# Graph attention and graph convolution on one core: values by a second level of seven products, and two weights in one tile

## Chip, core and metric

The kernel runs on one core of a Trainium2 chip. The time is device microseconds of one execution; three runs are shown. A profile of one more execution gives the trace.

## What is computed

```python
# x: (32, 512, 512) f32, adj: (512, 512) of 0 and 1, weights (512, 512), 8 heads of 64
def attention(x):
    q, k, v = x @ Wq + bq, x @ Wk + bk, x @ Wv + bv      # split into 8 heads
    scores = q @ k.T / sqrt(64) + where(adj == 0, -1e9, 0)
    return softmax(scores) @ v
def convolve(x):
    d = where(deg > 0, rsqrt(deg), 0)                     # deg: row sums of adj
    return (adj * d[:, None] * d[None, :]) @ (x @ weight) + bias
x = layernorm(x + attention(x))
x = layernorm(x + convolve(x))
```

Everything is float32. One of the 32 elements of the first axis is called a batch below.

## The kernel before

Every projection of a batch is a product of two 512 x 512 matrices, and each is made by seven products of their halves in place of eight (Strassen's scheme in Winograd's form). The tile `XT` (seven parts of 128 x 2 x 256, the 2 being two blocks of the contracted axis) holds the transposed x: parts 0 to 3 are its quadrants, parts 4 to 6 and a rewritten 2 are differences. `wk`, `wq`, `wv`, `w1` hold the weights in the same seven parts. `seven` (line 315) walks a table of steps: a bank of PSUM (region A, B or D), the numbers of the two parts, and the moves afterwards, either "put" (a copy to SBUF by ScalarE) or "add" (VectorE adds the bank to what lies in SBUF). A later step on the same region goes on adding up in the bank, so it must wait until the moves have read it. `values_of` (line 335) has one half product per step, four matmuls of 128 x 128 by 256 columns. `CHAIN` (line 288) is its table: products (0,0), (4,4), (5,5), (1,1), (6,6), (2,3), (3,2).

The order of instructions on each compute engine is written out by hand: `InOrder` (line 34) pins it, and `play(main, beside)` (line 104) runs one entry of `main`, which are matmul steps with their moves, and then the side work listed under its number. The DMAs of SP are issued through the scheduler, in order, and wait for what they need.

The main loop (line 777) handles batch b with its neighbours b+1 (projections), b-1 and b-2 (convolution and the second normalization):

- `stretch(b, one)`, line 452: scores of two head pairs (tile `sc`; VectorE masks into `e`, ScalarE takes the exponential in place), POOL's sums of numerators (`accumulate`, tile `acc`, three adds a head pair), then the product of numerators and values (`av`); VectorE transposes that into the one buffer `yb`, from which four DMAs fill `yT`. Eight tiles `e` rotate.
- keys and queries of b+1, two chains of seven steps taken in turn (`kq`), with beside them on POOL and ScalarE the second normalization's factors and output (`rstd`, `add`, then `y`, stored by SP) of b-2, and the first normalization of b-1.
- `stretch(b, two)` for the other two head pairs.
- `conv["first"]` of b-1 (adjacency by `hi` and `lo`), `values_of(b + 1)`, and `conv["second"]` of b-1, again seven half products. Beside them: `turn` (line 126) transposes x of b+2 into `XT` in two halves on VectorE; the first turn frees the x buffer, and `load_x` on SP then fetches the second half. `combine` (line 159) makes the four differences on POOL, and `bias_values` (line 357) adds the bias to the values on POOL. In this version POOL does the bias first and the differences afterwards.

Iterations 0, LAST-1 and LAST have orders of their own. `wv` and `wq` stand in tiles of their own for the whole kernel; late in the kernel free parts of them serve as scratch (lines 419, 485, 681).

Of the kernel before, what the change touches and what calls it, by code (L numbers as in the profile page):

```python
# [1 line left out]

# [15 lines left out]
P = 128  # L18
# [31 lines left out]
def unshifted(  # L50
# [24 lines left out]
    consts = ctx.enter_context(tc.tile_pool(name="consts", bufs=1))  # L75
    acts = ctx.enter_context(tc.tile_pool(name="acts", bufs=2))
    work = ctx.enter_context(tc.tile_pool(name="work", bufs=2))
    small = ctx.enter_context(tc.tile_pool(name="small", bufs=3))
    psum = {}

# [29 lines left out]

    X = {}
    columns = consts.tile([P, 12, 2, DT], F32, name="columns")
    XT = consts.tile([P, 7, 2, HALF], F32, name="xT")

    def load_x(b, j):
        if b == 1 and j == 1:
            X[b, j] = work.tile([P, 8, DT, 32], F32, name="x1", tag="e", bufs=8)
        else:
            X[b, j] = acts.tile([P, 8, DT, 32], F32, name="x", bufs=1)
        for q in range(4):  # L120
            nc.sync.dma_start(
                X[b, j][32 * q : 32 * (q + 1)],
                x[b, ts(j, HALF), ts(q, P)].rearrange("(k s) (t r) -> s k t r", s=32, r=32),
            )
# [34 lines left out]
    def combine(b, at):  # L159
        to, a, c = PARTS[at]  # L160
        engine = gpsimd if b else vector
        engine.tensor_tensor(XT[:, to], XT[:, a], XT[:, c], ALU.subtract)

    R = {}

# [42 lines left out]
    R[0] = acts.tile([P, NT, D], F32, name="xr", tag="zT", bufs=1)  # L208
    R[0] = [R[0][:, i, :] for i in range(NT)]

    wv = consts.tile([P, 7, 2, HALF], F32, name="wv")
    for i in range(2):
        for k, engine in enumerate((nc.sync, nc.scalar)):
            engine.dma_start(R[0][2 * i + k], x[0, ts(2 * i + k, P), :])
# [3 lines left out]
    wk = load_parts(Wk, "wk", nc.sync)  # L218
    bk_c = load_column(bk, 0)
    bq_c = load_column(bq, 1)  # L220
    wq = load_parts(Wq, "wq", nc.sync)
    adj_sb = acts.tile([P, NT, N], F32, name="yT")
    nc.sync.dma_start(adj_sb, adj.rearrange("(t p) o -> p t o", p=P))
    w1 = consts.tile([P, 7, 2, HALF], F32, name="w1")
    for i in range(2):
# [2 lines left out]
            W1[:, ts(i, HALF)].rearrange("(t p) o -> p t o", p=P),  # L228
        )
    b1_r = load_row(b1, "b1_r", nc.sync)  # L230
    load_x(1, 0)
    load_x(1, 1)

# [78 lines left out]
        ("A", (6, 6), (("add", (1, 1)), ("put", (1, 0)))),  # L312
        ("E", (3, 2), (("add", (1, 0)),)),
    )
    def seven(table, multiply, put, add):
        regions = {}

        def step(region, ij, moves):
            fresh = region not in regions
            if fresh:  # L320
                regions[region] = bank([P, 2, HALF])
            p = regions[region]
            multiply(p, *ij, fresh)
            for kind, q in moves:
                (put if kind == "put" else add)(q, p)

        return each(step, *table)
# [5 lines left out]
        vector.tensor_scalar(bias[:, 1], bq_c, SCALE, None, op0=ALU.mult)  # L333

    def values_of(b):
        def multiply(p, i, j, fresh):
            for r in range(2):
                for u in range(2):
                    tensor.matmul(
                        p[:, r, :], XT[:, j, u, ts(r, P)], wv[:, i, u, :],  # L340
                        start=fresh and r == 0 and u == 0, stop=u == 1, skip_group_check=True,
                    )

        def out(i, j):
            if b not in V:
                V[b] = acts.tile([P, NT, D], F32, name="v", bufs=1)
            return V[b][:, 2 * j : 2 * j + 2, ts(i, HALF)]

        def put(q, p):
            scalar.copy(out(*q), p)  # L350

        def add(q, p):
            vector.tensor_add(out(*q), out(*q), p)

        return seven(CHAIN if b else PLAIN_FIRST, multiply, put, add)

    def bias_values(b):
        for n in range(NT):
# [1 line left out]

    def keys_and_queries(b, r):
        def multiply(p, i, j, fresh):
            for c, w in enumerate((wk, wq)):
                for u in range(2):
                    tensor.matmul(
                        p[:, c, :], w[:, i, u, ts(r, P)], XT[:, j, u, :],
                        start=fresh and c == 0 and u == 0, stop=u == 1, skip_group_check=True,
                    )

        def out(i, j):  # L370
            if (b, ORDER[0]) not in KQ:
                for g in ORDER:
                    KQ[b, g] = acts.tile([P, 2, N], F32, name="kq", bufs=6)
            return KQ[b, r + 2 * i][:, :, ts(j, HALF)]

        def put(q, p):
            g = r + 2 * q[0]
            for c in range(2):
                scalar.activation(out(*q)[:, c], p[:, c], AF.Identity, bias=bias[:, c, g : g + 1], scale=1.0)

        def add(q, p):
            vector.tensor_add(out(*q), out(*q), p)

        return seven(CHAIN if b else PLAIN_FIRST, multiply, put, add)
# [5 lines left out]
    def scores(b, g):  # L390
        E[b, g] = []
        for j in range(NT):
            e = work.tile([P, 2, N], F32, name="e", bufs=8)
            E[b, g].append(e)
            p = pair("sc")
            for k in range(2):
                r = slice(k * HD, (k + 1) * HD)
                tensor.matmul(p[:, k, :], KQ[b, g][r, 0, ts(j, P)], KQ[b, g][r, 1, :], start=True, stop=True)
            vector.scalar_tensor_tensor(
                e, p, CUT, maskT[:, j, None, :].to_broadcast([P, 2, N]), op0=ALU.min, op1=ALU.subtract  # L400
            )
            scalar.activation(e, e, AF.Exp)

    def accumulate(b, g):
# [9 lines left out]
        for l in range(2):  # L414
            n = 2 * ORDER.index(g) + l
            if n < 2:
                a = work.tile([P, 2, N], F32, name="acc", bufs=2)
            else:
                t, at = ((XT, 0), (XT, 2), (XT, 4), (wv, 0), (wv, 2), (wv, 4))[n - 2]
                a = t[:, at : at + 2].rearrange("p k u o -> p k (u o)")  # L420
            gpsimd.tensor_add(a, e[2 * l], e[2 * l + 1])
            ACC[b, g].append(a)
# [53 lines left out]
    def sums(b, c, p):  # L476
# [5 lines left out]
                    start=k == 0, stop=k == len(parts) - 1,  # L482
                )
        if c == 0:
            SM[b] = wq[:, 6].rearrange("p u n -> p (u n)")
            vector.tensor_scalar(SM[b], p, 1e-36, None, op0=ALU.max)
        else:
            vector.scalar_tensor_tensor(SM[b], p, 1e-36, SM[b], op0=ALU.max, op1=ALU.add)
# [137 lines left out]
    def convolve(b):  # L626
# [48 lines left out]
        def multiply(p, i, j, fresh):  # L675
            if "y" not in t:
                if last:
                    t["y"] = [work.tile([P, 2, D], F32, name="y2", tag="e", bufs=8) for _ in range(2)]
                else:
                    if b == LAST - 2:  # L680
                        y = wq[:, :NT].rearrange("p k u o -> p k (u o)")
                    else:
                        y = acts.tile([P, NT, D], F32, name="y", tag="lo", bufs=1)
                    t["y"] = [y[:, 2 * k : 2 * k + 2, :] for k in range(2)]
# [9 lines left out]
        def move(q, p, to):  # L694
            if not aside:
                vector.tensor_add(of(t["y"], *q), to(*q), p)
                return
            side = work.tile([P, 2, HALF], F32, name="side", tag="e", bufs=8)
            scalar.copy(side, p)
            extend.append(lambda: gpsimd.tensor_add(of(t["y"], *q), to(*q), side))  # L700

# [54 lines left out]
    turn_first(1, 0)  # L756
    turn_first(1, 1)
    run(v[1:5])
    scalar.activation(wq[:, :4], wq[:, :4], AF.Copy, scale=SCALE)
    weigh(wk, gpsimd)  # L760
    run(v[5:])
    biases()
    wq_parts = each(lambda k: weigh_part(wq, vector, k), *range(4))
    kq = keys_and_queries(0, 0)
    run(wq_parts[:2] + kq[:1] + wq_parts[2:3] + kq[1:2] + wq_parts[3:] + kq[2:])
    bias_values(0)
    play(keys_and_queries(0, 1), {
        1: [lambda: adjacency(0)], 3: [lambda: turn(1, 0), lambda: adjacency(1)],
# [1 line left out]
    turn(1, 1)  # L770
    for k in range(4):
        combine(1, k)

    f, c = {}, {}
    for b in range(B):
# [13 lines left out]

        def turns(b=b + 2):
            if b >= B:
                return [], []
            return [lambda: turn(b, 0)], [lambda: turn(b, 1)] + [lambda k=k: combine(b, k) for k in range(4)]

        fold0, fold1 = folds(one) if b < LAST else ([], [])
        rest = back["measure"][3:] + back["root"] if back else []
# [21 lines left out]
        else:  # L820
# [5 lines left out]
                3: conv["parts"][1:] + e["inverse0"] + ahead["grow"],  # L826
            })

        stretch(b, two, f[b]["pairs"][0] + f[b]["pairs"][1] if b == LAST else ())

        fold0, fold1 = folds(two) if b < LAST else ([], [])
        turn0, turn1 = turns()
        if b < LAST:
            end = f[b]
            v, bias_v = values_of(b + 1), [lambda b=b + 1: bias_values(b)]
            if b == 0:
                play(v, {
                    1: fold0, 4: turn0 + fold1, 6: bias_v + turn1,
                })
            else:  # L840
                conv = c[b - 1]
                main = conv["first"] + v + conv["second"]
                grow, parts, scale = ahead["grow"], conv["parts"], end["scale"]
                if b < LAST - 1:
                    beside = {
                        1: parts[:1] + fold0, 3: parts[1:], 4: fold1, 5: grow[:1], 6: grow[1:2] + end["inverse"],
                        7: grow[2:3] + scale[:1], 8: grow[3:] + scale[1:2] + turn0, 9: scale[2:3],
                        10: scale[3:] + bias_v, 12: turn1,
                    }
                else:  # L850
                    measure, norm, low = end["measure"], end["norm"], end["low"]
                    beside = {
                        0: [lambda: load_residual(LAST - 1)], 1: parts[:1] + fold0, 3: parts[1:], 4: fold1,
                        5: grow[:1] + end["inverse"], 6: grow[1:2] + scale[:2], 7: grow[2:3] + scale[2:] + end["add"],
                        8: grow[3:], 9: measure[:1], 10: measure[1:2] + bias_v, 11: measure[2:3],
                        12: measure[3:] + end["root"], 13: norm[:1], 14: norm[1:2] + low[:1], 15: norm[2:3] + low[1:2],
                        16: norm[3:] + low[2:3], 17: low[3:] + end["lift"],
                    }
                play(main, beside)

# [311 lines left out]
```

## Time and profile before

| | us |
|---|---|
| median of 3 runs | 2747.85 (2747.67 to 2747.91) |
| profiled execution | 2747.42 |
| its span, first to last instruction | 2745.6 |
| mean granted TensorE clock | 0.998 |
| busy TensorE, VectorE, POOL, ScalarE | 2720.6, 1890.6, 1792.8, 1260.1 |

In the profile PE is TensorE's matmul side and PEld its weight loads; DVE is VectorE, ACT ScalarE, POOL GpSimd, SP the engine that issues DMAs. All instructions that go through the recording helper carry its line, 44, so groups are told apart by their tiles, written out<-in. A float32 matmul appears as two records, a float32r matmul (`hi`, `lo`) as one. In a timeline the columns are start, length, engine, line, operation, tiles, shape and count, and in brackets the idle time before and what ended it. Matmuls overlap, so the pace is the distance between starts, not the length of one. DMA moved 141.04 MB at a mean of 51 GB/s.

### The profile page before, as it was taken

The page shows a single profiled execution, that of the slowest core. Times are in us where ns is not written, and L with a number is a line of the kernel's source. Part 1 is how long each engine was busy: PE and PEld are TensorE (multiplying, and loading weights), DVE is VectorE, ACT ScalarE, POOL GpSimd, SP SyncE. Part 2 cuts the span into 40 slices and gives each one's busy share as a digit, 9 for nine tenths or more (in the row PEclk, how much of TensorE's full clock was granted, in tenths as well). Part 3 has the DMA queues.
Part 4 walks back from the last instruction along what each step waited for, and adds up shares of the span by engine and source line. Part 5 has one row for each costly group of instructions (what it writes and reads, how often), then busy time and mean ns, then how long its engine had stood idle before and what let it go on. Part 6 is the DMA issues. An engine that isn't in the chain of part 4 may idle for free.

```text
span 2745.6 us, 34622 instructions
## 1 busy us (share of the span) xinstructions
PE 2720.6 (99%) x12540; PEld 1900.4 (69%) x12540; DVE 1890.6 (69%) x2685; ACT 1260.1 (46%) x1807; POOL 1792.8 (65%) x1176
## 2 busy tenths in 40 slices
PE   9999999999999999999999999999999999999997
PEld 6676676776766766767667677676676676766765
DVE  4777766667666667666777666766666766677667
ACT  3335444454444454444544445444445544454444
POOL 4666667567676666666666756667666666667665
PEclk9999999999999999999999999999999999999999
DMA  4111221112121111211122211212111121112211
GB/s 127 31 28 46 58 58 47 54 39 54 54 62 39 45 48 54 62 43 45 45 58 58 50 50 39 54 55 62 39 46 47 54 62 43 48 41 58 64 38 47
DMA packets 379107, 141.04 MB, mean 51 GB/s; under 512 B 277808, under 2 KB 345392, under 8 KB 378928
## 3 DMA queue, kind: packets, MB, share of 16 engines
q1 hardware_dynamic: 377776, 137.17, 19.0%
q8 instruction: 101, 1.65, 0.3%
q10 hardware_dynamic: 1152, 1.57, 0.2%
q14 instruction: 78, 0.64, 0.1%
HBM read 71.83 MB, written 33.55 MB: 38 GB/s over the span
## 4 chain that ended last, share of the span: by engine, by line
PE 97%; DVE 2%; ACT 0%; DMA 0%; issue 0%; POOL 0%; SPq 0%; DVEq 0%; POOLq 0%; ACTq 0%
PE mm L44 64%; PE sc L44 16%; PE av L44 16%; DVE xT L44 0%; DVE st L44 0%; DVE yT L44 0%; DMA xr<-in_x_dram 0%; POOL y L44 0%; ACT yT L44 0%; ACT hi L44 0%; DVE y L44 0%; DMA x<-in_x_dram 0%; DVE mv L44 0%; DVE folded L44 0%; DVE acc L44 0%
## 5 line engine op out<-in xcount | busy, mean ns | idle before, releaser
L44 ACT ACTIVATE e<-e 128x1024 f32<-128x1024 f32 x512 | 541.1, 1057 | 493.2 <-DVE e L44 460.0
L44 DVE SCALAR_TENSOR_TENSOR e<-sc,maskT 128x1024 f32<-128x1024 f32 x512 | 584.8, 1213 | 107.5 <-PE sc L44 107.5
L44 POOL TENSOR_TENSOR acc<-acc,e 128x1024 f32<-128x1024 f32 x248 | 589.3, 2376 | 19.4
L44 PE MATMUL mm<-xT,wk 128*128 128x256 f32 x1792 | 463.2, 381 | 0.3 <-DVE kq L44 0.3
L44 PE MATMUL sc<-kq 64*128 64x512 f32 x2048 | 459.7, 597 | 1.8 <-DVE e L44 1.4
L44 PE MATMUL mm<-xT,wq 128*128 128x256 f32 x1792 | 459.9, 379 | 0.0
L44 PE MATMUL av<-e,v 128*64 128x512 f32 x2048 | 453.6, 595 | 0.3
L44 POOL TENSOR_TENSOR acc<-e 128x1024 f32<-128x1024 f32 x126 | 298.0, 2366 | 233.7 <-ACT e L44 233.7
L44 PE MATMUL mm<-wv,xT 128*128 128x256 f32 x1792 | 398.1, 380 | 0.6 <-DVE xT L44 0.6
L44 PEld LDWEIGHTS mm<-xT,wk 128*128 128x128 f32 x1792 | 337.5, 190 | 70.5 <-DVE mv L44 23.5
L44 PEld LDWEIGHTS mm<-xT,wq 128*128 128x128 f32 x1792 | 340.5, 190 | 46.3
L44 PEld LDWEIGHTS mm<-wv,xT 128*128 128x128 f32 x1792 | 338.0, 190 | 47.9 <-issue 1.4
L44 PEld LDWEIGHTS sc<-kq 64*128 64x128 f32 x2048 | 191.5, 186 | 238.1 <-issue 175.1
L44 PEld LDWEIGHTS av<-e,v 128*64 128x64 f32 x2048 | 145.0, 137 | 301.4 <-issue 264.4
L44 ACT ACTIVATE kq<-mm,bias 128x256 f32<-128x256 f32 x512 | 214.5, 473 | 284.6 <-PE mm L44 284.4
L44 POOL TENSOR_TENSOR v<-v,bv_r 128x512 f32<-128x512 f32 x128 | 161.3, 1288 | 239.2 <-ACT v L44 236.5
L44 POOL TENSOR_TENSOR yT<-yT,b_r 128x512 f32<-128x512 f32 x126 | 156.9, 1278 | 241.1 <-DVE lo L44 241.1
L44 DVE STREAM_TRANSPOSE yb<-av 128x512 f32<-128x512 f32 x127 | 91.1, 717 | 253.9 <-DMA yT<-yb 202.9
L44 PE MATMUL mm<-w,zT 128*128 128x256 f32 x992 | 229.6, 379 | 0.0
L44 PEld LDWEIGHTS mm<-w,zT 128*128 128x128 f32 x992 | 188.3, 190 | 26.6 <-issue 1.1
L44 PE MATMUL mm<-adjT,hi 128*128 128x512 f32 x512 | 201.5, 397 | 0.8 <-ACT side L44 0.8
L44 PE MATMUL mm<-adjT,lo 128*128 128x512 f32 x512 | 197.8, 390 | 0.0
(121 smaller groups left out, 3000.0 us busy)
## 6 DMA issues: line engine op xcount, KB each, us to landing
yT<-yb SPq DMA_DIRECT2D x508, 64.0 KB, 2.3
x<-in_x_dram SPq DMA_DIRECT2D x248, 128.0 KB, 2.5
out_dram<-y SPq DMA_DIRECT2D x123, 256.0 KB, 2.0
xr<-in_x_dram SPq DMA_DIRECT2D x118, 256.0 KB, 3.3
wk<-in_x_dram SPq DMA_DIRECT2D x8, 256.0 KB, 2.8
wk<-in_L_gnn_Wk_dram SPq DMA_DIRECT2D x8, 128.0 KB, 4.5
wq<-in_L_gnn_Wq_dram SPq DMA_DIRECT2D x8, 128.0 KB, 3.1
yT<-in_adj_dram SPq DMA_DIRECT2D x1, 1024.0 KB, 6.9
```

What stands on the lines that cost most here:

```text
L44: return self.tc.keep_in_program_order(op(*args, **kwargs))
```

## The change

In batches 1 to 31 the four half products (1,1), (3,2), (2,3), (4,4) of the values are each made by seven products of quarters. One leaf step does the same quarter product of all four, as four matmuls of 128 x 128 by 128 columns, into one bank. Three half products, (0,0), (5,5), (6,6), follow as before (`OUTER`), now all as adds. The product (4,4) has to reach two quadrants, which one add on POOL does (`spread_last`).

For that, x needs four more parts of quarters (`quarter`, on POOL, four adds a batch, `XT` grows from 7 to 11 parts), and the weights need three (`weigh_quarters`, once, at the start). The seven parts of `wv` and of `wq` are written to DRAM once and share the tile `wqv`: `swap(1)` loads the values' weights after the keys and queries, `swap(0)` brings the queries' back after the values. The eight numerators become one tile `NUM`, taken in the same rotation; its first four slots hold `wv` during the start. Turns, combinations, quarters and bias adds take new places, and `conv["second"]` is interleaved with the last values' steps.

```diff
+    def numerators():
+        return NUM[:, next(taken) % 8]
+    def quarter(at):
+        old, new = XT[:, 1:5].rearrange("p k u (t o) -> p k u t o", t=2), QUARTERS
+        to, a, c = (
+            (1, old[:, :, 0, 1], old[:, :, 0, 0]), (2, old[:, :, 1, 1], new[:, 1]),
+            (3, old[:, :, 1, 1], old[:, :, 0, 1]), (0, old[:, :, 1, 0], new[:, 2]),
+        )[at]
+        gpsimd.tensor_tensor(new[:, to], a, c, ALU.subtract)
...
+    def swap(k):
+        nc.sync.dma_start(wqv, stored[k])
...
+    LEAF = tuple(CHAIN[k] for k in (0, 1, 3, 2, 5, 4, 6))
+    OUTER = (
+        ("A", (0, 0), (("add", (0, 0)),)),
+        ("A", (5, 5), (("add", (0, 1)),)),
+        ("A", (6, 6), (("add", (1, 1)), ("add", (1, 0)))),
+    )
...
+        def multiply_quarters(p, i, j, fresh):
+            for n, (k, l) in enumerate(((1, 1), (3, 2), (2, 3), (4, 4))):
+                right = w[:, k, i % 2, ts(i // 2, P)] if i < 4 else wv_quarters[:, i - 4, k - 1]
+                left = XT[:, l, j % 2, ts(j // 2, P)] if j in (0, 1, 3) else QUARTERS[:, max(j - 3, 0), l - 1]
+                tensor.matmul(p[:, n, :], left, right, start=fresh and n == 0, stop=True, skip_group_check=True)
+        def put_quarters(q, p):
+            out(0, 0)
+            scalar.copy(quarter_of(*q), p.rearrange("p (j i) o -> p j i o", i=2))
+        def add_quarters(q, p):
+            to = quarter_of(*q)
+            vector.tensor_add(to, to, p.rearrange("p (j i) o -> p j i o", i=2))
+        def spread_last():
+            gpsimd.tensor_add(out(0, 1), out(0, 1), out(1, 1))
...
-        return seven(CHAIN if b else PLAIN_FIRST, multiply, put, add)
+        if b == 0:
+            return seven(PLAIN_FIRST, multiply, put, add)
+        leaf = seven(LEAF, multiply_quarters, put_quarters, add_quarters, (4, P))
+        return leaf + [spread_last] + seven(OUTER, multiply, put, add)
...
+    weigh_quarters(gpsimd)
+    nc.sync.dma_start(stored[1], NUM[:, :4].rearrange("p e k (u o) -> p (e k) u o", u=2)[:, :7])
+    nc.sync.dma_start(stored[0], wqv)
     bias_values(0)
...
-            return [lambda: turn(b, 0)], [lambda: turn(b, 1)] + [lambda k=k: combine(b, k) for k in range(4)]
+            return [lambda: turn(b, 0)], [lambda: turn(b, 1)], [lambda k=k: combine(b, k) for k in range(4)] + [quarters]
...
+        if b < LAST:
+            swap(1)
         stretch(b, two, f[b]["pairs"][0] + f[b]["pairs"][1] if b == LAST else ())
...
+            back_to_queries = [lambda: swap(0)] if b < LAST - 1 else []
             if b == 0:
                 play(v, {
-                    1: fold0, 4: turn0 + fold1, 6: bias_v + turn1,
+                    1: fold0, 4: fold1, 8: turn0, 9: turn1, 10: combined + back_to_queries + bias_v,
                 })
...
-                main = conv["first"] + v + conv["second"]
+                second = conv["second"]
+                k = 6 if b < LAST - 1 else 8
+                main = conv["first"] + v[:k] + second[:1] + v[k:9] + second[1:2] + v[9:10] + second[2:3] + v[10:] + second[3:]
...
-                        1: parts[:1] + fold0, 3: parts[1:], 4: fold1, 5: grow[:1], 6: grow[1:2] + end["inverse"],
-                        7: grow[2:3] + scale[:1], 8: grow[3:] + scale[1:2] + turn0, 9: scale[2:3],
-                        10: scale[3:] + bias_v, 12: turn1,
+                        1: parts[:1] + fold0, 3: parts[1:], 5: fold1, 6: grow[:1], 8: grow[1:2], 9: grow[2:3] + end["inverse"],
+                        10: grow[3:] + scale[:1], 11: scale[1:2], 13: turn0 + scale[2:3], 14: scale[3:],
+                        16: turn1, 17: combined[:2], 18: combined[2:] + back_to_queries + bias_v,
```

Iteration LAST-1 gets a new list of side work in the same manner, with `k` 8 in place of 6. The scratch that lay in `wv` and `wq` moves to `wqv` and, for the second convolution of batch LAST-2, to the quarters' parts of `XT`.

## Prediction

> **What bounds the kernel now.** I read the page first, then TensorE's timeline of one batch, then those of the other engines over the same batch.
>
> ```profile
> span 2745.6 us, 34622 instructions
> PE 2720.6 (99%) x12540; PEld 1900.4 (69%) x12540; DVE 1890.6 (69%) x2685; ACT 1260.1 (46%) x1807; POOL 1792.8 (65%) x1176
> PE 97%; DVE 2%; ACT 0%; DMA 0%; issue 0%; POOL 0%; SPq 0%; DVEq 0%; POOLq 0%; ACTq 0%
> L44 PE MATMUL mm<-wv,xT 128*128 128x256 f32 x1792 | 398.1, 380 | 0.6 <-DVE xT L44 0.6
> L44 PEld LDWEIGHTS mm<-wv,xT 128*128 128x128 f32 x1792 | 338.0, 190 | 47.9 <-issue 1.4
> ```
>
> TensorE sets the end (97% of the chain of waits); every other engine has idle time. A float32 product is two records, so 1792 is 32 batches of 7 products of 4 matmuls. A mean of 380 ns is a latency; the pace must come from the spacing in TensorE's timeline:
>
> ```profile
> 39.59 1.04 PE L44 MATMUL mm<-ident,yT 128*128 128x128 f32 x8
> 40.47 1.03 PE L44 MATMUL mm<-xT,wk 128*128 128x256 f32 x4
> ...
> 134.75 0.38 PE L44 MATMUL mm<-folded,spread 128*128 128x128 f32 x2
> 134.97 1.03 PE L44 MATMUL mm<-xT,wk 128*128 128x256 f32 x4
> ...
> 1193.47 5.34 PE L44 MATMUL mm<-wv,xT 128*128 128x256 f32 x24
> 1198.65 0.38 PE L44 MATMUL mm<-folded,spread 128*128 128x128 f32 x2
> ```
>
> From 1193.47 to 1198.65, 24 records of 256 columns: 0.216 us each, a half product of 8 records 1.727. Records of 128 columns: 0.88/8 = 0.110 (transposes), 0.22/2 = 0.110 (folded).
>
> Batches repeat every 84.42 us. I give times of a batch from S, the start of the first stretch's scores (1217.96). Keys and queries start at S+14.08. The change loads POOL, which ScalarE waits for, so these rows (POOL, then ACT) matter most:
>
> ```profile
> 1206.64 4.99 POOL L44 TENSOR_TENSOR v<-v,bv_r 128x512 f32<-128x512 f32 x4 [7.89 <-ACT v L44]
> 1211.58 5.20 POOL L44 TENSOR_TENSOR xT<-xT 128x512 f32<-128x512 f32 x4
> 1222.71 2.37 POOL L44 TENSOR_TENSOR acc<-e 128x1024 f32<-128x1024 f32 x1 [5.94 <-ACT e L44]
> ...
> 1237.26 1.02 POOL L44 TENSOR_TENSOR rstd<-ve,minus_half 128x4 f32<-128x4 f32 x1
> 1238.36 0.20 POOL L44 TENSOR_TENSOR add<-nmu,rstd 128x4 f32<-128x4 f32 x1
> ```
>
> ```profile
> 1238.59 0.81 ACT L44 ACTIVATE y<-y,add,rstd 128x512 f32<-128x512 f32 x1 [1.95 <-POOL add L44]
> 1239.31 0.82 ACT L44 ACTIVATE kq<-mm,bias 128x256 f32<-128x256 f32 x2
> ...
> 1242.15 0.84 ACT L44 ACTIVATE kq<-mm,bias 128x256 f32<-128x256 f32 x2
> ```
>
> POOL is free from 1216.78 (S-1.2) to 1222.71 (S+4.75), then sums numerators without a break, then makes the norm factors. ScalarE stands 1.95 us for them, with the bank copies of keys and queries queued behind. The third copy of the first chain ends at 1242.99 (S+25.03). Its bank is needed again by that chain's fifth product, the ninth step, which TensorE starts at 1245.96 (S+28.0). The slack is 2.95 us.
>
> **The change, part by part.**
>
> *Smaller products.* Out go 4 half products a batch: 32 x 0.216 = 6.91 us. In come 7 x 4 matmuls, 56 records x 0.110 = 6.16. That is -0.75 us in each of batches 1 to 31, -23 us in all. No row has 56 such records in line. From below I take 0.109, from above the mean weight load of 190 ns, as if no load overlapped more than its neighbour; I take 0.110, since the folded pair has real float32 loads of 190 ns and still keeps 0.110. The Trainium skill ("TensorE: Matmul & The Clock Gate", section "Back-to-back issue gap") speaks against this part: it gives a sustained 81 ns for a pair of weight load and matmul at 128 columns, where the stream alone would be about 56. An estimate by that ratio is 0.155 us a record here, 8.7 us a batch, a loss of 1.8; the two rows at 0.110 don't agree with it, but they are short.
>
> *Moves out of PSUM.* The seven small products have 4 copies on ScalarE (0.59) and 3 adds on VectorE (0.69), as CHAIN had; the three outer ones add 4 adds on VectorE, 2.6 us. A small product takes 0.88 us of TensorE, so a bank is wanted back sooner. The closest is the seventh after the sixth on the same bank: the add is done 0.27 + 0.65 us after the sixth, and a `second` product of 1.73 us stands between. Hidden. In batch LAST-1 nothing stands between but the folded pair: about 0.8 us, once.
>
> *Weights in turn.* Two DMAs of 1.8 MB a batch, on SP. The adjacency (1 MB) took 6.9 us beside other loads; by that, 12 us. Values may wait 14.2 + 7.2 us after the last query product, the queries 6.9 + 14.1 after the last value product, iteration 0 has 14.2. Hidden; from above, twice as slow, 3 us late at each swap. Behind the swap on SP stand yT<-yb (issued 11.5 us after a stretch's start) and x loads for the next round; neither is short of time. The numerators keep their ring of eight.
>
> *POOL and the order of turns.* This decides. Before, the bias adds (4) and combinations (4) ran from S-11.3 to S-1.2. Now both x turns come later: turn one after the first outer product, turn two after the third of the `second` products. Behind turn two stand on POOL 4 combinations, 4 quarters and 4 bias adds; the spread add goes into idle time. The turns wait for each other through the load of the second half of x, which SP issues when turn one has freed the buffer. In iteration 0 that load ended the wait:
>
> ```profile
> 113.49 1.24 DVE L44 STREAM_TRANSPOSE xT<-x 128x1024 f32<-128x1024 f32 x1
> ...
> 118.87 1.25 DVE L44 STREAM_TRANSPOSE xT<-x 128x1024 f32<-128x1024 f32 x1 [1.17 <-DMA x<-in_x_dram]
> ```
>
> 4.14 us lie between the end of one and the start of the other. After the first outer product TensorE still has eight products of 1.727 and 0.1 us to S, so it ends at S-13.9. Its add waits 0.27 and takes 0.6; turn one ends 1.24 later, at S-11.8; turn two starts 4.14 later and ends at S-6.4; POOL starts at S-6.3. Behind turn two on VectorE stand the last outer product's adds and the next `second` adds; no bank of theirs is wanted for two products (3.5 us).
>
> A POOL add of 512 elements runs 1.27, one every 1.235, or 1.345 behind its own result (the four xT: 5.20). Twelve, five of them behind a result, take 15.4 us to the start of acc: S+9.1 instead of S+4.75, 4.35 late. For the quarters, four runs of 128, the nearest rows are 1.27 (whole) and 1.42 (y<-y,side, two runs of 256, mean); nothing is below. I take 1.27; 1.42 adds 0.6 us. The bias adds end at S+5.4 to S+9.1, one every 1.24; the attention product starts at S+7.1 and needs the last of them at S+9.7: free by 0.6. But acc, rstd and add are POOL's own line, so ScalarE's store starts 4.35 later, the third copy ends at S+29.4, and TensorE, ready at S+28.0, waits **1.4 us a batch**. After that the chain recovers: the last low part ends at S+39.4, b1's adds at S+44.4, as the second stretch's acc starts (S+44.6).
>
> So a batch changes by -0.75 + 1.43 = +0.68.
>
> *Iteration 0*, with no `second` to stand between: VectorE ends the second yb at 106.5, folds to 109.0, adds twice to 110.1, folds to 112.5, adds to 113.1. The seventh small product starts then instead of at 109.1. Scores start at 119.3 (116.16 before); turn one ends 117.9, turn two 123.3; POOL's twelve run 123.4 to 138.8, so the last values of the first head pair end at 139.7, of the second at 143.3. Keys start there instead of 132.92: +10.4, less 0.75 in the next values: +9.6 once.
>
> *Startup*: the weights' quarters (4 adds, 5 us) lie in POOL's idle 20.3 us before 52.8; quarters of batch 1 delay acc by 5 there, with 13 us idle behind. Nothing.
>
> **Sum.** 9.6 + 28 x 0.68 (iterations 2 to 29) + 1.5 (iteration 30: 0.68 and 0.8) = +30. The span becomes 2775.6, and with the 1.8 us around it (profiled execution 2747.42) 2777.5; the median of the runs is 0.4 above that execution.
>
> **Rivals.**
> - *The gain comes through.* POOL's line reaches ScalarE less than 2.95 us late, for instance if the quarters take 0.9 us or the x load lands sooner. For it: 35% of POOL is idle. Against: the rows above. 9.6 + 0.8 - 29 x 0.75 = -11.4: 2736. The kernel is faster than before from a line 1.05 us shorter on (a wait under 0.39), and all of it is there at 1.4.
> - *The line is longer.* Quarters of 1.43 us (the mean of w<-w, POOL's slowest adds of this size) and an x load 1.2 us later, 1.8 us more a batch: +50, about 2828. For it: a line without slack passes every delay on.
> - *Weight loads bind.* 56 x 0.19 = 10.6, +3.7 a batch in place of -0.75, about 2907. Or the swaps land 3 us late twice a batch, about 2950. Against: 0.110, and 20 us of cover.
> - *The change does less than it says*: a wait of 0.3 to 0.65 instead of 1.43, near 2750, so that gain and waits cancel.
>
> **How the numbers follow.** Forecast 0.58 (2764 to 2800: quarters at 1.42 give +17, and the start of the line, which rests on one load's 4.14 us, may be 0.2 to 0.45 us off, 6 to 13 us in 29 batches); gain comes through 0.20; near 2750 0.07; longer line 0.10; weight loads or swaps 0.05. Less or more than 0.2% (5.5 us) is about what a measurement of this kernel can tell from no change: faster 0.20, same 0.07, slower 0.73. The range 2734 to 2805 leaves out part of the first rival, most of the longer line and the last.
>
> **What would show it.** In TensorE's timeline the small products at 0.88 us each; POOL's acc at S+9; ScalarE's first y near S+25; a gap of about 1.4 us in TensorE before the ninth step of keys and queries, put down to ScalarE's kq; batches 85.1 us apart; iteration 0's values with a wait of 4 us. Wrong if that gap is missing, or if gaps stand before the first value or query product (DMA), or the small products are wider than 0.9 us.

## The result, and the profile after

| | before | after |
|---|---|---|
| median of 4 runs each, us | 2747.88 (2747.67 to 2748.88) | 2786.28 (2785.86 to 2788.38) |
| profiled execution, its span, us | 2747.42, 2745.6 | 2788.38, 2786.6 |
| mean granted TensorE clock | 0.998 | 0.995 |

The ratio is 1.0141 [1.0123, 1.0158]: the kernel became 38 us slower, where 30 were forecast. The profiled execution of after is the longest of its four runs, 2.1 us over their median, so the account below, made against it, explains 41 us. 1.2 of them lie behind TensorE's last product, at the very end of that execution, as is said further down.

The page of after, in the places that answer to those of before: span, busy times, chain by engine, and the groups of the first key products and of the values.

```profile
span 2786.6 us, 36220 instructions
PE 2717.3 (98%) x13284; PEld 1907.6 (68%) x13284; DVE 1972.3 (71%) x2809; ACT 1257.0 (45%) x1807; POOL 1999.4 (72%) x1335
PE 76%; DVE 8%; POOL 5%; ACT 4%; DMA 3%; SPq 2%; issue 1%; ACTq 0%; DVEq 0%; POOLq 0%
L45 PE MATMUL mm<-xT,wk 128*128 128x256 f32 x1792 | 466.5, 383 | 32.5 <-ACT kq L45 32.5
L45 PE MATMUL mm<-wqv,xT 128*128 128x128 f32 x1736 | 304.8, 322 | 5.8 <-DVE v L45 5.8
```

TensorE still sets the end, but its part of the chain fell from 97% to 76%: other engines now end waits that it stands in. One row says which. The products of keys and queries stood 32.5 us for ScalarE's `kq`, and the view of waits counts them:

```profile
PE mm L45 <- ACT kq L45: 32.5, 29, 1.6
```

29 times, once a batch. The next three views, POOL, ScalarE and TensorE, follow one such wait back to its start. They are timelines of the batch whose first scores start at S = 1242.03.

```profile
1235.84 10.38 POOL L45 TENSOR_TENSOR xT<-xT 128x512 f32<-128x512 f32 x8 [7.04 <-DVE xT L45]
1246.17 4.98 POOL L45 TENSOR_TENSOR v<-v,bv_r 128x512 f32<-128x512 f32 x4
1251.11 2.37 POOL L45 TENSOR_TENSOR acc<-e 128x1024 f32<-128x1024 f32 x1
...
1266.59 0.20 POOL L45 TENSOR_TENSOR add<-nmu,rstd 128x4 f32<-128x4 f32 x1
```

```profile
1266.83 0.81 ACT L45 ACTIVATE y<-y,add,rstd 128x512 f32<-128x512 f32 x1 [6.11 <-POOL add L45]
1267.55 0.82 ACT L45 ACTIVATE kq<-mm,bias 128x256 f32<-128x256 f32 x2
...
1270.38 0.84 ACT L45 ACTIVATE kq<-mm,bias 128x256 f32<-128x256 f32 x2
```

```profile
1269.17 1.03 PE L45 MATMUL mm<-xT,wqv 128*128 128x256 f32 x4
1271.28 1.13 PE L45 MATMUL mm<-xT,wk 128*128 128x256 f32 x4 [1.08 <-ACT kq L45]
```

POOL waits 7.04 us for the second x turn, starts its twelve adds at S-6.2 and reaches `acc` at S+9.1 without a pause. `add` comes 4.2 us later than before, ScalarE stands 6.11 us for it (1.95 before) in front of its first `y`, the third copy ends at S+29.2, and TensorE, ready at S+28.0, waits. The step after the wait starts its records a little further apart as well (1.13 in place of 1.03 for the group).

The shift of after against before, by stage, in the two profiled executions:

| | forecast | measured |
|---|---|---|
| to the first scores of iteration 2 | +9.6 | +14.0 |
| 28 batches (iterations 2 to 29) | +19.0 | +23.0 |
| iteration 30 to the end | +1.5 | +3.9 |
| sum | +30 | +41 |

### The profile page after: what moved, and what is told of

The parts are those of the page before. It is cut to its first block, busy times and chain, and to the rows that moved or that the text cites. A ratio compares the mean times of both kernels' runs of the same rounds, so it can differ in the third digit from the quotient of the medians.

```text
span 2786.6 us, 36220 instructions
## 1 busy us (share of the span) xinstructions
PE 2717.3 (98%) x13284; PEld 1907.6 (68%) x13284; DVE 1972.3 (71%) x2809; ACT 1257.0 (45%) x1807; POOL 1999.4 (72%) x1335
## 4 chain that ended last, share of the span: by engine, by line
PE 76%; DVE 8%; POOL 5%; ACT 4%; DMA 3%; SPq 2%; issue 1%; ACTq 0%; DVEq 0%; POOLq 0%
PE mm L45 48%; PE sc L45 15%; PE av L45 13%; POOL acc L45 2%; ACT kq L45 2%; DMA yT<-yb 2%; SPq L512 2%; ACT y L45 1%; DVE yb L45 1%; DVE folded L45 1%; DVE acc L45 1%; DVE ve L45 1%; POOL rstd L45 1%; POOL xT L45 1%; DVE st L45 1%
## 5 line engine op out<-in xcount | busy, mean ns | idle before, releaser
L45 PE MATMUL mm<-xT,wk 128*128 128x256 f32 x1792 | 466.5, 383 | 32.5 <-ACT kq L45 32.5
L45 POOL TENSOR_TENSOR xT<-xT 128x512 f32<-128x512 f32 x250 | 314.2, 1273 | 243.2 <-DVE xT L45 233.4
L45 PE MATMUL mm<-xT,wqv 128*128 128x256 f32 x1792 | 459.9, 379 | 0.0
L45 PEld LDWEIGHTS mm<-xT,wqv 128*128 128x128 f32 x1792 | 340.5, 190 | 46.3
L45 PE MATMUL mm<-wqv,xT 128*128 128x128 f32 x1736 | 304.8, 322 | 5.8 <-DVE v L45 5.8
L45 PEld LDWEIGHTS mm<-wqv,xT 128*128 128x128 f32 x1736 | 263.4, 192 | 30.0 <-issue 4.6
L45 DVE TENSOR_TENSOR v<-v,mm 128x512 f32<-128x512 f32 x221 | 147.5, 679 | 151.0 <-PE mm L45 146.3
L45 DVE STREAM_TRANSPOSE acc<-acc 128x1024 f32<-128x1024 f32 x124 | 152.6, 1231 | 77.1 <-POOL acc L45 76.8
## 6 DMA issues: line engine op xcount, KB each, us to landing
x<-in_x_dram SPq DMA_DIRECT2D x244, 128.0 KB, 3.2
```

The costliest lines, as they stand in the source:

```text
L45: return self.tc.keep_in_program_order(op(*args, **kwargs))
```

## The experiments

Theory: POOL's line between the second x turn and `acc` has become longer than the slack that ScalarE and the banks of keys and queries leave, and what is over goes to TensorE's wait before the ninth step, batch by batch; the first values of iteration 0 add a once-only cost. Rivals: POOL's load as such, the swaps of weights, the pace of the small products. Every ratio is to the kernel before, run on the same chip.

**The quarters made later** (`e1_quarters_late`): the same four adds, after the norm factors instead of ahead of `acc`.

```diff
-            return ..., [lambda k=k: combine(b, k) for k in range(4)] + [quarters]
+            return ..., [lambda k=k: combine(b, k) for k in range(4)]
-                        7: weights[2:3], 8: exact[2:3], 9: weights[3:], 10: exact[3:],
+                        7: weights[2:3], 8: exact[2:3], 9: weights[3:] + [quarters], 10: exact[3:],
-                        4: store[3:] + measure[:2], 5: measure[2:] + ahead["root"], 7: ...
+                        4: store[3:] + measure[:2], 5: measure[2:] + ahead["root"] + [quarters], 7: ...
```

> The four quarters adds of each batch leave POOL's line ahead of acc and run during keys and queries of the same XT, after rstd and add of the first normalization, where POOL stood idle 7.6 us; all work is kept. Theory (POOL's line of twelve makes ScalarE late, and TensorE waits for ScalarE): the line shrinks by 5.1 us, acc starts near S+4.8, the gap before the ninth step of keys and queries is gone, batches 83.85 us apart (84.43 - 0.60), iteration 0 about 5 us shorter; about 2744 us. Rival 1 (the swaps or the small products themselves hold things up): nothing moves but a little of the start, 2775 or more. Rival 2 (POOL's total load counts, not the place): within 10 us of the changed kernel's 2786.

Measured: 2741.95 us, ratio 0.9979 [0.9970, 0.9989]. POOL's timeline in the batch with S = 1219.03:

```profile
1218.01 4.96 POOL L45 TENSOR_TENSOR v<-v,bv_r 128x512 f32<-128x512 f32 x4
1223.73 2.37 POOL L45 TENSOR_TENSOR acc<-e 128x1024 f32<-128x1024 f32 x1 [0.77 <-ACT e L45]
```

The bias adds are done 0.77 us before the exponentials are there, so `acc` starts at S+4.7 (4.8 before the change), and the ninth step starts at S+28.0 with no wait. POOL's busy time rose all the same, from 1999.4 to 2028.8 us. Its load isn't the cause; the place of four adds is.

**Only the fourth quarter made later** (`e2_one_late`).

```diff
-        for at in range(4):
+        for at in range(3):
             quarter(at)
+    def last_quarter():
+        quarter(3)
-                        ..., 5: measure[2:] + ahead["root"], 7: ...
+                        ..., 5: measure[2:] + ahead["root"] + [last_quarter], 7: ...
```

> One of the four quarter adds (the fourth) is made while keys and queries run, after acc and the norm factors; the other three stay ahead of acc. Theory (a threshold: the wait before the ninth step is what POOL's line is longer than the slack): the line is one add shorter, 1.24 to 1.35 us, so acc starts near S+7.7, the third copy of the first chain ends near S+27.8, and the wait of 1.15 us is gone in ordinary batches; 0.1 to 0.7 us of it is left in the about five batches whose x load lands late. The gain of 0.60 a batch then comes through in iterations 2 to 29: 15 to 17 us of loss less 23 to 25 in after, about 2750 to 2755 us (the start and the tail still cost 14 and 4). Rival (POOL's load as such slows the kernel, in proportion): a quarter of what moving all four gave, 44.3/4 = 11 us, about 2775.

Measured: 2750.15 us, ratio 1.0006 [0.9997, 1.0016]. `acc` starts at S+7.8, the third copy ends at S+28.0, and the whole row of 32.5 us has shrunk, in the waits of this kernel, to

```profile
PE mm L45 <- ACT kq L45: 2.2, 5, 0.6
```

One add of 1.27 us a batch is worth 36 us here: a threshold, not a load.

**Two quarters made twice** (`e6_two_more`): the second and third are computed again, with the same values.

```diff
-        for at in range(4):
+        for at in (0, 1, 2, 3, 1, 2):
```

> The first two quarter adds after the first are made twice, with the same values: two more adds in POOL's line ahead of acc. Theory: there is no slack left in the line, so each add goes over to TensorE's wait before the ninth step in full: the wait grows from 1.15 to 3.6 to 3.85 us, acc starts near S+11.5, batches are 2.5 to 2.7 us longer, 29 batches give 72 to 78, and with 2.5 in iteration 0 the kernel takes 2860 to 2868 us; the bias adds, the last of which then ends near S+11.6, may also hold the first attention product (S+7 to S+10), which would show as a wait of av for POOL's v and would not add to the other. Rival (the wait is ScalarE's own order or the banks, not the length of the line): the wait stays near 1.15 us and the kernel near 2786 to 2795.

Measured: 2867.68 us, ratio 1.0435 [1.0419, 1.0451]. The median batch went from 85.16 to 87.72 us, 1.28 for each add. TensorE in the batch with S = 1279.64:

```profile
1288.90 1.08 PE L45 MATMUL av<-e,v 128*64 128x512 f32 x4 [0.16 <-POOL v L45]
...
1295.82 1.13 PE L45 MATMUL mm<-xT,wk 128*128 128x256 f32 x4
...
1311.43 1.13 PE L45 MATMUL mm<-xT,wk 128*128 128x256 f32 x4 [1.53 <-ACT kq L45]
```

The keys now start at S+16.2 instead of S+14.1, held by the bias adds, and the ninth step at S+31.8: of the 3.8 us by which it is late, 2.1 are lost at the attention products, ahead of the keys, and 1.7 at the step itself (1.53 of them idle). POOL's line is 2.6 us longer than in after and 2.1 of that are lost ahead of the keys, so the bias adds were in time by about 0.5 us; the prediction had 0.6.

**ScalarE's stores placed behind the copies** (`e3_stores_behind`): POOL's line as it is, but ScalarE no longer waits for it ahead of the bank copies.

```diff
-                    0: rest + scale + ahead["add"], 1: store[:1] + fold0, 2: store[1:2], 3: store[2:3] + fold1,
-                    4: store[3:] + measure[:2], 5: measure[2:] + ahead["root"], 7: ...
+                    0: rest + scale + ahead["add"], 1: fold0, 3: fold1,
+                    4: measure[:2], 5: store + measure[2:] + ahead["root"], 7: ...
```

> The changed kernel with POOL's line left as it is, but ScalarE's four output activations y moved from behind steps 2 to 5 of keys and queries to behind step 6, so that no bank copy of the first three pairs stands behind them. Theory (the link from POOL to TensorE is ScalarE's queue): acc still starts near S+9, the gap before the ninth step is gone, batches 83.9 us apart; with the start left as it is about 2750 us. Rival (VectorE or the values pass POOL's lateness on as well): a gap of 0.5 us or more moves to another place, 2765 or more.

Measured: 2746.33 us, ratio 0.9995 [0.9986, 1.0005]. ScalarE in the batch with S = 1224.32:

```profile
1247.35 0.84 ACT L45 ACTIVATE kq<-mm,bias 128x256 f32<-128x256 f32 x2 [0.83 <-PE mm L45]
1249.08 0.84 ACT L45 ACTIVATE kq<-mm,bias 128x256 f32<-128x256 f32 x2 [0.89 <-PE mm L45]
1249.80 2.92 ACT L45 ACTIVATE y<-y,add,rstd 128x512 f32<-128x512 f32 x4
```

`acc` is as late as in after (S+9.0), yet ScalarE's copies wait only for TensorE, and the wait is gone. With the two kernels above this closes the chain: late POOL, ScalarE's queue, bank, TensorE. Over the last four kernels and the two at hand, medians over the batches, in us from S:

| kernel | acc starts | third copy ends | ninth step | batch |
|---|---|---|---|---|
| before | 4.8 | 25.0 | 28.0 | 84.42 |
| after | 9.0 | 29.2 | 29.2 | 85.16 |
| one quarter late | 7.8 | 28.0 | 28.0 | 83.94 |
| all quarters late | 4.7 | 25.0 | 28.0 | 83.88 |
| two more | 11.6 | 31.7 | 31.8 | 87.72 |
| stores behind | 9.0 | 23.9 | 28.0 | 83.82 |

**The swaps alone** (`e4_swaps_alone`): half products and the orders of before, with the shared tile and both swaps a batch.

```diff
-        leaf = seven(LEAF, multiply_quarters, put_quarters, add_quarters, (4, P))
-        return leaf + [spread_last] + seven(OUTER, multiply, put, add)
+        return seven(CHAIN if b else PLAIN_FIRST, multiply, put, add)
...
-                        16: turn1, 17: combined[:2], 18: combined[2:] + back_to_queries + bias_v,
+                        10: back_to_queries + scale[3:] + bias_v, 12: turn1,
```

> Only the shared weight tile with its two swaps a batch (and the numerators' one tile): values by seven half products as before, no quarters, all orders as before. Theory (the 1.8 MB loads take about 7.5 us inside 20 us of cover): same as before, 2747 to 2750 us. Rival (the swaps cost, by their own time or by delaying x and yb transfers): 2755 or more, with gaps before the first value or query products or late turns.

Measured: 2747.70 us, ratio 1.0000 [0.9990, 1.0009]; both stretches of a batch keep their length (38.46 and 45.96). Sixty-one loads of 1792 KB, 112 MB, cost nothing.

**Another order in iteration 0** (`e5_first_values`): bias ahead of the second x turn, differences last.

```diff
-                    1: fold0, 4: fold1, 8: turn0, 9: turn1, 10: combined + back_to_queries + bias_v,
+                    1: fold0, 6: fold1, 8: turn0, 10: back_to_queries + bias_v + turn1 + combined,
```

> The changed kernel with another order in iteration 0 alone: the second fold after the sixth small product, both turns' side work at the end with the bias adds ahead of the second turn, combinations and quarters. Theory (iteration 0 lost about 14 us to VectorE's order and to values that waited for POOL's line): keys of iteration 1 start about 12 to 14 us sooner, about 2773 us, batches unchanged at 85.1 us. Rival (the loss at the start is the swap's or the small products'): 2782 or more.

Measured: 2779.72 us, ratio 1.0115 [1.0098, 1.0131]. The keys of iteration 1 start 12.7 us sooner than in after, counted from the first scores of iteration 0 (134.40 for 147.63 from the start of the span), but only 6.6 are kept at the end. TensorE there:

```profile
134.40 1.13 PE L45 MATMUL mm<-xT,wk 128*128 128x256 f32 x4
...
160.35 2.05 PE L45 MATMUL mm<-xT,wk 128*128 128x256 f32 x4 [4.74 <-DVE kq L45]
162.19 1.91 PE L45 MATMUL mm<-xT,wqv 128*128 128x256 f32 x4
```

A wait of 4.74 us for VectorE, and behind it groups of 4 records spaced 1.8 us in place of 0.86: TensorE at half its clock (the granted clock is 0.50 from 159.5 to 166.4). No step of the prediction had a price for that. In after, TensorE's timeline has two such gaps, in iterations 0 and 1:

```profile
108.80 1.13 PE L45 MATMUL mm<-wv_quarters,xT 128*128 128x128 f32 x8
113.51 5.46 PE L45 MATMUL mm<-wqv,xT 128*128 128x128 f32 x16 [3.58 <-DVE v L45]
119.82 1.99 PE L45 MATMUL mm<-wqv,xT 128*128 128x256 f32 x8 [0.85 <-DVE v L45]
...
138.07 9.63 PE L45 MATMUL av<-e,v 128*64 128x512 f32 x32 [4.92 <-POOL v L45]
```

The view of stretches gives the granted clock (the third number from the end) around them:

```profile
112.00:112.50 0.50, 0.00 (x0) 0.00 (x0) 0.50 (x1) 0.00 (x0) 0.00 (x0) 1.00 0.00 0
112.50:113.00 0.50, 0.00 (x0) 0.00 (x0) 0.50 (x2) 0.00 (x0) 0.00 (x0) 0.51 0.00 0
...
119.50:120.00 0.50, 0.18 (x1) 0.18 (x2) 0.50 (x2) 0.00 (x0) 0.00 (x0) 1.00 0.00 0
...
136.50:137.00 0.50, 0.00 (x0) 0.00 (x0) 0.00 (x0) 0.48 (x1) 0.50 (x2) 0.50 0.00 0
...
143.50:144.00 0.50, 0.50 (x4) 0.14 (x2) 0.00 (x0) 0.00 (x0) 0.49 (x1) 1.00 0.00 0
```

The clock halves at 112.5 while TensorE stands, and stays halved well into the work, to 119.3; again from 136.4 to 143.2. The 32 attention records take 9.63 us where 7.09 is their usual time.

**The gaps filled with idle products** (`e9_filled`): the identity times itself, into banks that nobody reads, so that TensorE isn't idle in the two gaps.

```diff
+    def fill(p, n):
+        for k in range(n):
+            tensor.matmul(p[:, ts(k % 4, P)], ident, ident, start=True, stop=True)
...
+            if b == 1 and g == ORDER[0]:
+                fill(av, 18)
             values(b, g, av)
...
-                play(v, {
+                play(v[:6] + [lambda: fill(bank([P, N]), 12)] + v[6:], {
```

> As the changed kernel, but TensorE multiplies the identity by itself, 12 times (24 records of 128 columns, 2.7 us) ahead of the seventh small product of iteration 0 and 18 times (4.0 us) ahead of the first attention product of iteration 1, into banks that nobody reads; no result is touched. Theory (what iteration 0 lost beyond the prediction is mostly TensorE's clock, which falls to half in its two gaps of 3.58 and 4.92 us and stays there for 5 to 6 us of work): with the gaps filled the clock stays at 1.00; the 16 records from the seventh small product on take 2.9 us in place of 5.46, the first attention products 7.1 in place of 9.63, the scores of iteration 1 start 2.6 us sooner than in the changed kernel, and its keys and queries about 5 us sooner; since POOL and VectorE come only 2.6 us sooner, up to half of that may be lost again before the ninth to thirteenth step of keys and queries; the kernel gains 2.5 to 5 us: 2781 to 2784. Rival (the slow stretch is contention for the banks or weight loads while VectorE and POOL work): both groups stay as long as they were, and the kernel at 2786 or a little above.

Measured: 2783.25 us, ratio 1.0133 [1.0117, 1.0148]; the intervals of this and of after overlap, so the verdict is the trace's. TensorE in iterations 0 and 1:

```profile
108.91 2.84 PE L45 MATMUL mm<-ident 128*128 128x128 f32 x24
112.66 2.86 PE L45 MATMUL mm<-wqv,xT 128*128 128x128 f32 x16 [0.91 <-DVE v L45]
...
132.13 4.29 PE L45 MATMUL av<-ident 128*128 128x128 f32 x36
136.34 7.09 PE L45 MATMUL av<-e,v 128*64 128x512 f32 x32
```

5.46 became 2.86, and 9.63 became 7.09, with the clock at 1.00 in both groups: the clock it was, not banks or weight loads. Counted from the first scores of iteration 0, those of iteration 1 start 2.6 us sooner than in after, as expected. Its keys start 3.4 us sooner, not 5, and the scores of iteration 2 come 2.7 sooner. One reason lies in the scores between the two fillers:

```profile
124.22 7.97 PE L45 MATMUL sc<-kq 64*128 64x512 f32 x28 [1.96 <-DVE v L45]
```

They start sooner and so wait longer for VectorE (1.96 us, 1.00 in after), and the clock falls there, from 124.6 to 128.0. So the clock did not stay full throughout, as had been expected of it.

**Both cures** (`e7_both`: the quarters later, and the other order in iteration 0), then **an earlier end** (`e8_both_tail`: in iteration LAST-1 the side work of the normalizations one entry sooner).

```diff
-                        ... 10: grow[2:3] + scale[:2], 11: grow[3:] + scale[2:] + end["add"],
-                        14: measure[:1], 15: measure[1:2], 16: measure[2:3], 17: measure[3:] + end["root"], ...
+                        ... 9: end["inverse"] + scale[:1], 10: grow[2:3] + scale[1:3], 11: grow[3:] + scale[3:] + end["add"],
+                        13: measure[:1], 14: measure[1:2], 15: measure[2:3], 16: measure[3:] + end["root"], ...
```

> Quarters made while keys and queries run, and in iteration 0 the values' bias before the last x turn and the four differences. Theory: the two causes are separate, so the effects add: the gain of 0.55 a batch as with the quarters late, and the start shorter by the 6.6 us that the other order of iteration 0 saved: about 2735 to 2738 us, second stretch of scores of iteration 2 at +1 to +3 against before. Rival (what the first order saves in iteration 0 is lost again in iteration 1, where the quarters now stand beside keys and queries): within 2 us of the quarters late alone, 2740 to 2744.

> As the kernel with both edits, and in iteration LAST-1 the side work of the two normalizations (scale, measure, root, norm, low) stands one entry earlier. Theory: the 1.4 us that TensorE waited there for VectorE's low parts (the scores of the second pair of the last iteration) goes, and most of the tail's loss with it: 1 to 3 us below the kernel with both edits, about 2733 to 2737. Rival (the tail's loss lies in the outer products' shared bank and the last values, not in VectorE's low parts): no difference, within 0.5 us.

Measured: 2737.90 us, ratio 0.9965 [0.9952, 0.9979], and 2736.79, 0.9959 [0.9945, 0.9973]: both faster than the kernel before, by 10 and 11 us. The two effects add, although the start keeps 4.6 us of loss where 1 to 3 were expected: a wait of 3.08 us in iteration 1 halves the clock again. The end is told by TensorE's scores in the last iteration, of the first of these kernels and then of the second:

```profile
2643.01 3.70 PE L45 MATMUL sc<-kq 64*128 64x512 f32 x16
2648.13 4.52 PE L45 MATMUL sc<-kq 64*128 64x512 f32 x16 [1.41 <-DVE e L45]
```

```profile
2643.89 7.70 PE L45 MATMUL sc<-kq 64*128 64x512 f32 x32
```

The wait of 1.41 us is gone, and of the 1.7 us that the kernel with both edits lost between these scores and the end against before, none is left in the other (-0.25). The iteration before them became 0.3 us longer by it, and so 1.7 us are gained in all.

**The best kernel with its gap filled** (`e10_filled_best`): the same filler ahead of the thirteenth step of keys and queries of iteration 1.

```diff
+            if b == 1:
+                main = main[:12] + [lambda: fill(bank([P, N]), 12)] + main[12:]
             play(main, beside)
```

> As the kernel with both edits and the earlier tail, and the same filler (12 products of the identity, 2.7 us) in iteration 1 ahead of the thirteenth step of keys and queries, where TensorE waits 3.08 us for VectorE's kq and then works at half clock for about 3.3 us. Theory: the clock stays full, that step and the next take 0.86 us a half product again, and the kernel gains 1.3 to 1.7 us: about 2735 us. Rival (VectorE's kq adds, not the clock, set the pace there): nothing changes, within 0.4 us.

Measured: 2736.01 us, ratio 0.9962 [0.9948, 0.9975], which can't be told from 0.9959. TensorE:

```profile
155.46 2.84 PE L45 MATMUL mm<-ident 128*128 128x128 f32 x24
158.67 1.10 PE L45 MATMUL mm<-xT,wk 128*128 128x256 f32 x4 [0.37 <-DVE kq L45]
159.61 1.03 PE L45 MATMUL mm<-xT,wqv 128*128 128x256 f32 x4
```

The step runs at full clock, and the second stretch of iteration 1 starts 1.55 us sooner, counted from the first scores. But 0.6 of that is lost again by iteration 2 and 0.5 more by iteration 30; 0.4 us reach the end. So the clock was right, and that its gain would come through was wrong; what takes it back was not followed further.

## Why the prediction was right, and where it fell short

2777.5 us was forecast and 2786.28 measured, within the range. The mechanism is the one that was worked out, and it is shown: take away either of two links (the adds' place, ScalarE's order) and the loss in the batches goes. In the ordinary batches two small errors nearly cancel, which is luck: the gain was put 0.15 us a batch too high, and the wait 0.1 to 0.2 too high as well. So these batches (all but five of the 28) changed by +0.70 on the mean, and +0.68 was forecast.

- **POOL's line.** `acc` at S+9.1 was forecast and S+9.0 came, from 15.3 us of twelve adds, 1.27 for each quarter in spite of its four runs of 128. The third copy ended at S+29.2 (29.4 forecast); the ninth step starts 1.2 us late (1.43), of which the row counts 1.1 as idle, and with the slower start behind it the stretch is 1.31 us longer (38.46 to 39.77). The slack of 2.95 is borne out by the kernel with one quarter late, whose third copy ends 2.9 us later than before and whose ninth step is 0.01 late.
- **The small products.** -0.75 us a batch was forecast, -0.60 came (45.96 to 45.36). TensorE's timeline of after shows the pace:

```profile
1303.31 1.05 PE L45 MATMUL mm<-wqv,xT 128*128 128x128 f32 x8
1304.20 1.06 PE L45 MATMUL mm<-wv_quarters,xT 128*128 128x128 f32 x8
1305.09 1.06 PE L45 MATMUL mm<-wqv,xT 128*128 128x128 f32 x8
```

  0.893 us for 8 records, 0.1116 each where 0.110 was taken; by that 56 records save 0.66; the other 0.06 was not followed. The Trainium skill ("TensorE: Matmul & The Clock Gate", section "Back-to-back issue gap") gives 81 ns sustained for a pair of weight load and matmul at this width, against about 56 for a matmul taken alone. Here 40 records in line hold 0.1116, within 2% of the short rows of before, so the measurement speaks against a loss of that kind for float32. (From 0.110 that ratio makes 0.159 us a record and a loss of 2.0 a batch, a little more than the estimate in the prediction.)
- **The swaps and copies out of PSUM** were costed at nothing. The swaps cost nothing (ratio 1.0000); they land in a median of 7.5 us, where 12 were estimated. For the adds out of PSUM that end the values' steps TensorE waits in iterations 0 and LAST-1 alone, 0.56 us in the latter, where 0.8 was forecast.
- **"It rests on one load's 4.14 us."** In ordinary batches it is 4.1 to 4.3; in five of 28 it is 4.6 to 5.0. VectorE's turns in such a pair of batches, the first ordinary and the second late:

```profile
887.80 1.24 DVE L45 STREAM_TRANSPOSE xT<-x 128x1024 f32<-128x1024 f32 x1
893.20 1.25 DVE L45 STREAM_TRANSPOSE xT<-x 128x1024 f32<-128x1024 f32 x1 [0.20 <-DMA x<-in_x_dram]
```

```profile
972.88 1.24 DVE L45 STREAM_TRANSPOSE xT<-x 128x1024 f32<-128x1024 f32 x1
...
979.08 1.25 DVE L45 STREAM_TRANSPOSE xT<-x 128x1024 f32<-128x1024 f32 x1 [1.00 <-DMA x<-in_x_dram]
```

  Turn two starts 5.40 us after turn one in the first, 6.20 in the second, and a line without slack hands all of it to TensorE: 0.4 to 0.8 us in each of the five batches, 3.4 in all, most of the 4 us by which the 28 batches were mis-sized. Why the load is late there stays open.
- **Iteration 0, "+9.6 once".** The wait of 4 us before the seventh product came as 3.58. Two terms were missing. The three outer products share one bank with nothing between them, so TensorE waits 0.85 us twice (the wait that was costed at "about 0.8 us, once", in LAST-1, comes here too). The other is the clock, which by the kernel with its gaps filled is worth 2.6 us ahead of the scores of iteration 1 and 2.7 by iteration 2. Together they make the 4.4 us that were missing, if the two waits come through whole, which no run shows apart.
- **Iteration 30 and the end.** 1.5 forecast, 3.9 measured. Iteration 30 itself is only 0.6 us longer. 2.2 lie in the scores of the last iteration: VectorE's low parts come late there, which no step of the prediction looked at; placed one entry sooner they cost nothing (the last two kernels). The remaining 1.2 lie behind TensorE's last product, where the final rows are normalized and stored: 15.4 us to the end of the span in this execution of after, 14.3 in that of before, 13.8 to 14.6 in all other kernels, those with all of after's work among them. So this part most likely belongs to the one execution, not to the change.
- **The rivals.** "The gain comes through" was right in its mechanism: with the quarters later it does, 0.54 us a batch. The point from which it expected a faster kernel, a line 1.05 us shorter, was too near: with the line 1.2 us shorter the kernel stands at 2750, level with before, since the start costs 13.4 us and not 9.6, and a batch gains 0.40 on the mean and not 0.75. Weight loads, swaps and a still longer line are refuted, the last because 1.27 was the right row. A wait of 0.3 to 0.65 us, the fourth rival, was not met either: it is 1.2.

## What to carry to other kernels

An engine that is idle 35% of the time can still be full in the one window that matters: before adding work to it, write down its line from the last thing that it must wait for to the first thing that another engine waits for, and compare it with the slack there; past it, each add costs its full length in every batch. Here moving four adds behind the norm factors turned 1.4% slower into 0.2% faster. And a TensorE gap of 2 us or more may cost more than itself: the clock can be halved behind it for 3.4 or 6.8 us.

## What the runs showed of the hardware that was not expected

- **The clock.** The gaps of 3.06 to 7.48 us in iterations 0 and 1 all brought the granted clock to 0.50. Of the shorter ones, 2.22 us (quarters late) did not, 2.42 us (two quarters twice) and 1.96 us (gaps filled) did; none of 1.84 us or less did, in any of the kernels. TensorE's timeline and the clock in the kernel with two quarters twice:

```profile
89.01 1.10 PE L45 MATMUL mm<-xT,wk 128*128 128x256 f32 x4 [2.42 <-DVE kq L45]
89.95 1.62 PE L45 MATMUL mm<-xT,wqv 128*128 128x256 f32 x4
```

```profile
89.50:90.00 0.50, 0.50 (x4) 0.43 (x3) 0.50 (x1) 0.00 (x0) 0.00 (x0) 1.00 0.00 0
...
90.50:91.00 0.50, 0.50 (x3) 0.40 (x2) 0.50 (x2) 0.00 (x0) 0.00 (x0) 0.50 0.00 0
```

  The clock fell 1.2 us after TensorE had started again. In after it was low for 6.83 and 6.82 us, in the kernel with both cures for 3.4; and 17.07 us lie between the first rise (119.34) and the second fall (136.41) in after. These are multiples of 3.41. The Trainium skill ("TensorE: Matmul & The Clock Gate", section "What's actually happening") tells of such windows, 3413 ns long and running free of the kernel, with half rate after an idle one. The spacing agrees; "idle" has to be read widely. Taking the window as the 3.41 us before a fall, TensorE stood for 1.96 us of it in the filled kernel and 2.2 in the one with quarters twice; in the one with quarters late, counted on from its fall at 114.3, the gap of 2.22 us lies across two windows, at most 1.7 us in one. A fourth row narrows this: in the kernel with quarters twice TensorE stands from 1989.08 to 1990.92, 1.84 us that lie in one window, counted on from its falls, and the clock stays at 1.00. By these four rows the limit lies between 1.84 and 1.96 us of one window; more than four rows it is not.
- **Products of no use.** Records of the identity that nobody reads, put into a gap, kept the clock up behind it (12 products in 2.7 us). The trace shows the effect; the time at the end hardly does.
- **GpSimd.** A float32 add of 512 elements in four runs of 128 takes 1.27 us, as one of whole rows does.
